# One block around both layers, ordered with TimelineSim: a two-layer graph network on one core

## The chip, the cores and the metric

The kernel runs on one core of one Trainium2 chip. The metric is device time in microseconds of one execution. Five engines work in parallel, each through its own instructions in order: TensorE (PE, with its weight loads PEld), VectorE (DVE), ScalarE (ACT), GpSimd (POOL) and SyncE (SP). PE writes to PSUM, and the other engines move its results on. An engine whose next instruction waits for a semaphore holds up everything behind it in its own order.

## The reference, cut to what matters

The input x is 32 batches of 512 tokens with 256 features, adj a 0/1 matrix of 512 x 512 per batch, all float32 or int32. Two layers, each a graph step and a feed-forward step, each on a layer norm and added to its input:

```python
# layer 0
h = x @ W_msg;  msg = adj.T @ h / max(deg, 1)
x = x + relu(x @ W_upd + msg + bias)
t = max over features of (xf + Wt[u]) + bt          # 1024 outputs u
trop = s * max_p(t*sl_cvx + of_cvx) + (1-s) * min_p(t*sl_ccv + of_ccv)
out = (g*trop + (1-g)*gelu(xf @ Wc + bc)) @ Wd + bd # g = sigmoid(xf @ Wg + bg)
# layer 1
attention of 4 heads over adj;  x = x + norm(relu(att @ h + bias) + h)
sw = softmax((x @ W_x.T) @ W_slice.T / temp)        # 8 heads x 64 slices
st = (fx.T @ sw) / (sum(sw) + 1e-5)                 # 64 slice tokens of 512 features
ot = bidirectional state-space scan over the 64 slice tokens
x = x + (ot spread back by sw) @ out_w.T
```

(In the last lines x stands for the normed x where the reference norms it.)

## The kernel before, in words

`tile_kernel` (L2158) traces the whole program. Python generators yield after small pieces of work, and `woven` (L66) and a credit in layer 1 (L1595) interleave them, so that pieces of several batches are traced alternately. The traced order isn't yet the order of execution: the Tile scheduler takes the traced instructions of a block as a list in order of priority, runs them through a simulation of the machine, and writes for each engine the order in which that simulation issued them. Buffers of a pool and semaphores follow from that order. The kernel before gives no block of its own around the layers, so the scheduler's standard simulation orders them.

**Layer 0** is `layer0_sorted` (L98). In the front, about 330 us long, `features` prepares sorted weights while the first graph steps run. A graph step of one batch is `conv_in` (L386: ph L404) and `conv_out` (L412: pu L424, pm L434, and keep, the rows written for later). After every 8 batches (a segment of 4096 tokens), `put_in_order` (L473) sorts the tokens by how many features can decide their max-plus. `feed_forwards` (L543) then handles each segment in 8 groups of 512 sorted tokens, 32 groups in all: indirect DMAs on POOL gather the tokens (xs, L553) and rows of a table (L564, L595), DVE does the max-plus (L598), PE transposes xs and does clsp and gatep (L623), ACT turns them into cls and gate (L625), PE transposes the maxima (tz, L630), ACT and DVE build acc from tz (L632, L636, L637 to L641), and PE multiplies acc down (po, L652). The tiles clsp and gatep have two PSUM buffers between them, as do po with the graph steps, the transposes of xs, and tz. The graph steps of the next segment are woven in, and behind the last segment the setup and the first steps of layer 1.

**Layer 1** is `layer1_plain` (L865), with two streams.

- `attentions`: `prepare(b)` (L1148) gathers a batch, norms it, transposes it (x3T), computes heads (hp, L1180) and writes one row per head to DRAM (ownd, L1197, on SP), from where it is loaded to all partitions (own, L1200, on SP). `attention(b)` (L1216) forms the weights att on DVE (L1213) from own, other and mask, and multiplies them on PE (avp L1249, adp L1254); then norms the result (L1282 to L1300; mu goes through a power on POOL).
- `mixer(g)` for 16 groups of two batches. `slices` for each batch: lgp (L1335) and sw on ACT and DVE (L1336 to L1342), yTp (L1347), swp (L1352). `tokens` for both: uTp (L1366), rnp (L1372), scale on ACT (L1375), uT on DVE (L1379, L1381). `scan`: xp (L1400), bcp (L1409), dtp (L1428), zp (L1393); a convolution and activations on DVE and ACT; gp (L1487), segp (L1491, from seg, with decay = exp of it on ACT, L1493), xtp (L1496, copied to xk, L1498), qp (L1501); mix on DVE (L1505 to L1510); yp (L1517), y (L1522), yTp (L1527), yT (L1529), oTp (L1535), vp (L1557). `unslice`: outp (L1567), and the store of the batch.

The mixer of one group is one long chain of dependent steps through PE, ACT and DVE. Its counterpart, the attention of later batches, is traced between its steps by this credit:

```python
for want in mixer(g):
    credit += want * PACE
    while credit >= 1.0:
        credit -= 1.0
        if next(ahead, True):
            credit = 0.0
```

att has 13 buffers, own 5, x 5; the PSUM pool of layer 1 has 4 buffers for each of two tags (any for most, pv for the attention). After both layers come a sum of flags (L2196 to L2204) and a conditional branch to a general version of the layers, which isn't taken with these data.

Of the kernel before, what the change touches and what calls it, by code (L numbers as in the profile page):

```python
# [2156 lines left out]
@with_exitstack  # L2157
def tile_kernel(ctx, tc, ins, out):  # L2158
    nc = tc.nc
    cst = ctx.enter_context(tc.tile_pool(name="cst", bufs=1))  # L2160
    dram = ctx.enter_context(tc.tile_pool(name="dram", bufs=1, space=DRAM))
    ident = cst.tile([P, P], F32, tag="ident", name="ident")
    make_identity(nc, ident)
    eps = cst.tile([P, 1], F32, tag="eps", name="eps")
    nc.gpsimd.memset(eps, LN_EPS)
    eps2 = cst.tile([P, 2], F32, tag="eps2", name="eps2")
    nc.gpsimd.memset(eps2[:, 0:1], LN_EPS)
    nc.gpsimd.memset(eps2[:, 1:2], -0.5)

    def group(prefix):  # L2170
        return {k[len(prefix):]: v for k, v in ins.items() if k.startswith(prefix)}

    w0 = group("L0_gnn_") | group("L0_ffn_")
    w1 = group("L1_gnn_") | group("L1_ffn_")
    w1["gnn_bias"] = ins["L1_gnn_bias"]
    x2 = [dram.tile([N, D], F32, tag=f"x2_{b}", name=f"x2_{b}") for b in range(ins["x"].shape[0])]
    n0 = len(x2) * NT + w0["Wt"].shape[0] // P
    n1 = len(x2) * NT + 2 * w1["W"].shape[0] + 3
    again = cst.tile([1, 1], I32, tag="again", name="again")
    with tc.tile_pool(name="few", bufs=1) as few:  # L2180
        over = few.tile([P, n0 + n1], F32, tag="over", name="over")
        NSEG = 4
        x2s = [dram.tile([len(x2) // NSEG * N, D], F32, tag=f"x2s_{i}", name=f"x2s_{i}") for i in range(NSEG)]
        ranks = few.tile([P, len(x2) * NT], I32, tag="ranks", name="ranks")
        rest = []

        def following(ps):
            rest.append(layer1_plain(tc, ident, eps2, x2s, ranks, ins["adj"], w1, out, over[:, n0:], ps))
            return iter(lambda: next(rest[0]), True)

        layer0_sorted(tc, ident, eps2, ins["x"], ins["adj"], w0, x2s, ranks, over[:, :n0], following)
        for _ in rest[0]:
            pass


        ones = few.tile([P, 1], F32, tag="ones", name="ones")  # L2196
        nc.gpsimd.memset(ones, 1.0)
        worst = few.tile([P, 1], F32, tag="worst", name="worst")
        nc.vector.tensor_reduce(worst, over, AX.X, ALU.add)
        with tc.tile_pool(name="pf", bufs=1, space=PSUM) as ps:  # L2200
            pf = ps.tile([P, N], F32, tag="flag", name="flag")
            nc.tensor.matmul(pf[:1, :1], worst, ones, start=True, stop=True)
            nc.vector.tensor_copy(again, pf[:1, :1])
    rows = nc.values_load(again, min_val=0, max_val=4 * P * (n0 + n1))  # L2204
    with tc.If(rows > 0):
        layer0(tc, ident, eps, ins["x"], ins["adj"], w0, x2)
        layer1(tc, ident, eps, x2, ins["adj"], w1, out)
# [32 lines left out]
```

## Time and profile before

| | |
|---|---|
| median of 3 runs | 4462.75 us (4462.54 to 4462.93) |
| the profiled execution | 4459.08 us |
| its span on the core | 4456.4 us, so 2.7 us lie around it |
| mean granted TensorE clock | 0.948 of full speed |
| front, 0 to 330 us | PE busy 194.8 us |
| DMA over the span | 474.21 MB, mean 106 GB/s |
| layer 1's POOL mu L1300, 32 times | 111.6 us busy, 391.1 us idle before it for DVE |
| layer 0's DVE best L598, 212 times | 274.4 us busy, 121.9 us idle before it, most for ACT best L592 |

The profile shows one execution. A line of its timeline gives start and length in us, the engine, the line of the code, the operation, the tiles written and read, their shape and how often it stands in a run; the bracket behind it gives the idle time before it and what ended that. A line of the waits gives who waited for whom, the total in us, how often, and the longest.

### The profile page before, as it was taken

How to read it: one execution, taken by the hardware profiler on the slowest of the kernel's cores; microseconds unless marked ns; L12 is line 12 of the kernel's file. 1: busy time of each engine (PE TensorE's matmuls, PEld its weight loads, DVE VectorE, ACT ScalarE, POOL GpSimd, SP SyncE). 2: the span in 40 equal slices, each digit the busy share in tenths (PEclk: the TensorE clock that was granted, in tenths of full speed). 3: DMA queues.
4: the chain of work that ended last, by engine and by line, in shares of the span. 5: the costliest groups of instructions: out<-in, count | busy, mean ns of one | idle time of the engine just before them, and what ended most of it. 6: DMA issues, size and time to landing. Idle time of an engine off the chain costs nothing.

```text
span 4456.4 us, 57911 instructions
## 1 busy us (share of the span) xinstructions
PE 3922.0 (88%) x20311; PEld 2470.6 (55%) x20311; DVE 3347.2 (75%) x7008; ACT 2291.6 (51%) x4756; POOL 1718.8 (39%) x2036
## 2 busy tenths in 40 slices
PE   5568898899988999888997899999999999999987
PEld 4454565566656656545554455555555555555555
DVE  6668887897788987877766777767677877778763
ACT  3345565566564665556654544544545444454433
POOL 2357644664446644454314232332222232332220
PEclk8679999999999999989998999999999999999998
DMA  5546543664436543564422111111111111111100
GB/s 133 160 144 223 190 130 122 210 200 139 156 117 213 187 147 129 162 201 167 138 81 67 36 53 57 56 48 58 51 43 42 53 55 55 58 48 58 41 15 16
DMA packets 235107, 474.21 MB, mean 106 GB/s; under 512 B 38299, under 2 KB 114075, under 8 KB 234804
## 3 DMA queue, kind: packets, MB, share of 16 engines
q0 software_dynamic: 98688, 315.94, 22.2%
q1 hardware_dynamic: 136116, 154.46, 11.0%
q8 instruction: 162, 2.65, 0.2%
q14 instruction: 141, 1.16, 0.1%
HBM read 413.16 MB, written 57.16 MB: 106 GB/s over the span
## 4 chain that ended last, share of the span: by engine, by line
DVE 34%; PE 32%; DMA 11%; issue 9%; POOL 9%; ACT 5%; SPq 0%; POOLq 0%; DVEq 0%; ACTq 0%
DVE att L1213 5%; DVE acc L637 4%; PE clsp L623 3%; PE avp L1249 3%; PE po L652 3%; PE gatep L623 3%; DMA rows<-table,xs 2%; PE yTp L1347 2%; DVE sw L1337 2%; DVE sw L1342 2%; DVE best L598 2%; DMA rows<-table,tops 2%; DVE sst L1340 2%; DMA best<-table,xs 2%; PE xp L1400 1%
## 5 line engine op out<-in xcount | busy, mean ns | idle before, releaser
L623 PE MATMUL clsp<-xnT,wc 128*128 128x512 f32 x1024 | 520.8, 627 | 49.7 <-ACT cls L625 37.6
L623 PE MATMUL gatep<-xnT,wg 128*128 128x512 f32 x1024 | 499.8, 607 | 10.5 <-ACT gate L625 7.7
L652 PE MATMUL po<-wd,acc 128*128 128x256 f32 x2048 | 455.4, 381 | 6.1 <-DVE acc L641 3.8
L1213 DVE SCALAR_TENSOR_TENSOR att<-own,other,mask 128x512 f32<-128x512 f32 x512 | 392.9, 796 | 79.0 <-DMA own<-ownd 79.0
L652 PEld LDWEIGHTS po<-wd,acc 128*128 128x128 f32 x2048 | 388.3, 191 | 72.1 <-issue 9.2
L598 DVE SCALAR_TENSOR_TENSOR best<-rows,xs,best 128x1024 f32<-128x1024 f32 x212 | 274.4, 1295 | 121.9 <-ACT best L592 76.4
L637 DVE SCALAR_TENSOR_TENSOR acc<-past,fld,acc 128x512 f32<-128x512 f32 x448 | 345.7, 775 | 24.9 <-ACT past L636 16.9
L632 ACT ACTIVATE acc<-tz,fld 128x512 f32<-128x512 f32 x256 | 198.8, 777 | 269.3 <-PE tz L630 240.1
L623 PEld LDWEIGHTS gatep<-xnT,wg 128*128 128x128 f32 x1024 | 196.0, 196 | 252.3 <-issue 197.9
L636 ACT ACTIVATE past<-tz,fld 128x512 f32<-128x512 f32 x448 | 291.4, 693 | 68.1 <-DVE acc L637 66.6
L1347 PE MATMUL yTp<-sw,x 128*128 128x512 f32 x512 | 264.6, 655 | 64.3 <-DVE sw L1342 59.6
L595 POOL DMA_INDIRECT rows<-table,xs x212 | 249.5, 1177 | 171.6 <-DVE best L598 119.0
L1249 PE MATMUL avp<-att,hv 128*32 128x512 f32 x2048 | 298.9, 607 | 5.6 <-DVE att L1213 5.6
L623 PEld LDWEIGHTS clsp<-xnT,wc 128*128 128x128 f32 x1024 | 181.5, 198 | 188.1 <-issue 111.8
L434 PE MATMUL pm<-h,adj 128*128 128x258 f32 (+1 forms) x1024 | 181.2, 324 | 99.9 <-DVE keep L427 33.7
L1300 POOL TENSOR_TENSOR mu<-mu,eps 128x16 f32<-128x16 f32 x32 | 111.6, 3487 | 391.1 <-DVE mu L1299 391.0
L1335 PE MATMUL lgp<-wsl,x4T 128*128 128x512 f32 x512 | 242.8, 613 | 15.7 <-ACT sw L1336 6.8
L1154 POOL DMA_INDIRECT x<-x2s,ranks x128 | 135.9, 1062 | 298.1 <-DVE att L1213 148.1
L625 ACT ACTIVATE gate<-gatep,fld 128x512 f32<-128x512 f32 x256 | 175.5, 685 | 142.6 <-PE gatep L623 123.8
L553 POOL DMA_INDIRECT xs<-rows_of,order x128 | 156.1, 1219 | 221.5 <-DVE acc L637 100.8
L1567 PE MATMUL outp<-v,swT 128*128 128x256 f32 x1024 | 227.6, 381 | 0.0
L625 ACT ACTIVATE cls<-clsp,fld 128x512 f32<-128x512 f32 x256 | 176.1, 688 | 93.9 <-PE clsp L623 55.6
(599 smaller groups left out, 8978.1 us busy)
## 6 DMA issues: line engine op xcount, KB each, us to landing
adj<-in_adj POOLq DMA_DIRECT2D x128, 256.0 KB
ai<-in_adj SPq DMA_DIRECT2D x128, 256.0 KB
own<-ownd SPq DMA_DIRECT2D x128, 256.0 KB
rows_of<-keep SPq DMA_DIRECT2D x32, 550.0 KB
x<-in_x SPq DMA_DIRECT2D x32, 512.0 KB
x2s<-xs SPq DMA_DIRECT2D x32, 512.0 KB
out<-x SPq DMA_DIRECT2D x32, 512.0 KB
rows<-table,xs POOLq DMA_INDIRECT x212
```

Of the source, the lines that this page charges most:

```text
L595: nc.gpsimd.indirect_dma_start(out=row, out_offset=None, in_=table, in_offset=bass.IndirectOffsetOnAxis(ap=idxs[:, k : k + 1].bitcast(U32) ...
L598: nc.vector.scalar_tensor_tensor(m, row, vals[:, k : k + 1], m, ALU.add, ALU.max)
L623: nc.tensor.matmul(pf, wf[:, c, f * P : (f + 1) * P], xnT[:, c, :], start=c == 0, stop=c == DC - 1)
L625: nc.scalar.activation(o, pf, fn, bias=fld[:, f, bf : bf + 1], scale=1.0 if fn == AF.Gelu else 0.5)
L636: nc.scalar.activation(r, z, AF.Relu, bias=fld[:, f, AT + b : AT + b + 1])
L637: nc.vector.scalar_tensor_tensor(y, r, fld[:, f, CH + b : CH + b + 1], y, ALU.mult, ALU.add)
L652: nc.tensor.matmul(po[:, i, :], acc[f][:, t * P : (t + 1) * P], wd[:, f, :], start=f == 0, stop=f == FC - 1)
L1213: nc.vector.scalar_tensor_tensor(e, own[h], other[:, j, h : h + 1], mask[:, j, :], ALU.max, ALU.mult)
L1249: nc.tensor.matmul(pv[p][k * HW : (k + 1) * HW, :], hv[:, j, h, e : e + HW], weighed[b, h, j], **ends)
L1335: nc.tensor.matmul(pf, xnT[:, c, t * P : (t + 1) * P], wsl[:, c, :], start=c == 0, stop=c == DC - 1)
L1347: nc.tensor.matmul(py, xn[:, t, c * P : (c + 1) * P], sw[:, t, :], start=t == 0, stop=t == NT - 1)
L1567: nc.tensor.matmul(po[:, :D], swT[:, k, t * P : (t + 1) * P], v[:, k, :], start=k == 0, stop=k == KC - 1)
```

## The change: a block with another simulation

Both layers are traced inside one `tc.block`, which tells the scheduler to order it with TimelineSim, its more detailed simulator, in place of the standard one. What is traced, and in which order, is the same. The setup ahead of it (constants, the DRAM tiles) and the sum of flags behind it lie outside the block.

```diff
-        layer0_sorted(tc, ident, eps2, ins["x"], ins["adj"], w0, x2s, ranks, over[:, :n0], following)
-        for _ in rest[0]:
-            pass
-
+        with tc.block(schedule_with_timeline_sim=True):
+            layer0_sorted(tc, ident, eps2, ins["x"], ins["adj"], w0, x2s, ranks, over[:, :n0], following)
+            for _ in rest[0]:
+                pass
```

## The prediction

> **What bounds the kernel now.** I read the page's busy line first, then the chain, then busy time by stage, then what PE waits for in the steady part of layer 1, then single stretches of PE's timeline. From the page, and from the table by stages (columns: length, PE busy, PEld, DVE, ACT, POOL, PE clock, DMA share, GB/s):
>
> ```profile
> PE 3922.0 (88%) x20311; PEld 2470.6 (55%) x20311; DVE 3347.2 (75%) x7008; ACT 2291.6 (51%) x4756; POOL 1718.8 (39%) x2036
> DVE 34%; PE 32%; DMA 11%; issue 9%; POOL 9%; ACT 5%; SPq 0%; POOLq 0%; DVEq 0%; ACTq 0%
> ```
>
> ```profile
> 330.00:2375.00 2045.00, 1843.23 (x7181) 1181.03 (x7179) 1655.47 (x3053) 1198.60 (x2019) 1017.15 (x1254) 0.96 0.49 159
> ...
> 2534.00:4300.00 1766.00, 1643.19 (x10865) 985.75 (x10868) 1304.62 (x2811) 862.22 (x2205) 508.07 (x390) 0.98 0.16 50
> ```
>
> PE is the bound: layer 0 leaves it 2045.0 - 1843.2 = 202 us idle, the steady part of layer 1 only 1766.0 - 1643.2 = 123 us, about 9 us per group of two batches (the group from 3036.4 to 3162.7 takes 126.3 us, with PE busy for 116.8). The chain is spread over all engines, so PE's idle time is made of many short waits. No matmul is removed or added; so an order can only change these idle stretches, and the clock that follows them. PE's largest waits from 2560 to 4200, 13 groups (us in total, times, longest):
>
> ```profile
> PE yTp L1347 <- DVE sw L1342: 55.3, 31, 3.0
> PE oTp L1535 <- ACT yT L1529: 13.3, 14, 1.1
> PE rnp L1372 <- DVE mu L1293: 9.8, 12, 2.7
> ```
>
> The mixer's long chain (rnp, uT, xp, conv, gp, mix, yp, y) hardly appears here, because attention matmuls of the next batch stand between its hops. The last group has no next batch, so it shows the bare hops (start, length, and in brackets the idle time before):
>
> ```profile
> 4386.63 1.15 PE L1372 MATMUL rnp<-ident,rn 128*64 128x64 f32 x32
> 4390.43 5.44 PE L1400 MATMUL xp<-uT,inT 128*128 128x128 f32 x32 [2.65 <-DVE uT L1381]
> ...
> 4399.80 3.68 PE L1393 MATMUL zp<-inT,uT 128*128 128x512 f32 x8
> 4407.84 0.45 PE L1487 MATMUL gp<-cpad,bcT 64*64 64x64 f32 x8 [4.36 <-issue]
> 4408.23 1.87 PE L1491 MATMUL segp<-seg,seg_l 128*64 128x512 f32 x4
> ...
> 4416.13 3.28 PE L1517 MATMUL yp<-xk,mix 64*64 64x64 f32 x32 [3.48 <-DVE mix L1510]
> ```
>
> The same steps in a steady group have no idle before them and are shorter:
>
> ```profile
> 3162.67 3.84 PE L1400 MATMUL xp<-uT,inT 128*128 128x128 f32 x32
> ...
> 3180.01 0.46 PE L1487 MATMUL gp<-cpad,bcT 64*64 64x64 f32 x8
> 3180.39 1.42 PE L1491 MATMUL segp<-seg,seg_l 128*64 128x512 f32 x4
> ...
> 3188.86 1.90 PE L1517 MATMUL yp<-xk,mix 64*64 64x64 f32 x32
> ```
>
> **The change part by part.** I compared the built programs, engine by engine. The counted instructions and DMAs are the same one for one; 16 of 104 activation table loads go, each engine gets two branches, and waits are merged differently (more wait instructions on PE, DVE and ACT). So this is purely a question of order. I take the work between two steps in each order and price it by the rows of before.
>
> *Layer 1, per group.* In the new order nearly all attention matmuls of the group's second batch (about 25 us of PE work) stand ahead of uTp, inside the stretch where PE waited for sw; before, they stood behind it, between the mixer's hops. From this:
>
> - rnp to xp: filler 3.4 us before, none after (1.4 in every third group). The bare hop is 2.65 idle, so +2.65 or +1.25, on average 2.2.
> - zp to gp and segp: filler 6.6 before, 0.8 after. In the last group segp starts 12.36 us after xp's end (4395.87 to 4408.23); in a steady group zp ends 7.6 us after it (3166.51 to 3174.12). That leaves 4.75, less 0.8 filler and 0.46 for gp: 3.5. The new ACT order has one table load less here (1.28): 2.2. I take 2.8.
> - qp to yp: filler 5.8 before, 3.8 after, against a bare 3.48. The filler would cover it, but part of it is hp of the next batch, whose inputs are ACT copies now queued behind decay and xk. Ends 0 and 3.5; I take 2.0.
> - clock: in the last group xp takes 5.44 for 3.84 (+1.60), segp, xtp and qp 4.69 for 3.04 (+1.65), yp 3.28 for 1.90 (+1.38), at granted clocks 0.66 to 0.50. That is 4.6 if every hop lowers the clock and 0 if none does; I take half, 2.3.
> - own rows: att of the second batch (L1213) now stands on DVE ahead of half of the first's sw steps (L1337 to L1342). DVE waits at att for the DMA own<-ownd, 73.9 us in 13 groups, 5.7 each, so far with little of PE's behind it; now sw, and with it yTp, are queued behind. The queue on SP keeps its order. Ends 0 and 5.7; I take 4, since about half of sw has still to be done when the rows land.
> - saved: the waits for sw, 55.3 + 2.7 (L1341) over 13 groups, 4.5 each; and yTp, which took 7.56 us for 4.56 after such a wait in some groups (at clock 0.62), half of 3.0. Together 6.0. At the low end 7.5, at the high end 0, if the matmuls that fill the gap wait for own themselves.
>
> Sum: 2.2 + 2.8 + 2.0 + 2.3 + 4.0 - 6.0 = +7.3 per group, over 15 groups with a next batch +110 us. All low ends give 1.25 + 2.2 - 7.5 = -4.0, or -60 us; all high ends +20, or +300, which would need every bound at once.
>
> On the clock, the rows say this: gaps of 2.65 and 2.87 us were followed by 0.66 and 0.62, another gap of 2.87 by full speed (yTp in 4.56 us at 2771); hence the half. The Trainium skill, "TensorE: Matmul & The Clock Gate", section "Why this matters for your kernels", asks for no idle gaps over about 3 us between bursts; by that rule only the 3.48 and 4.36 gaps would cost clock, and xp's half of 1.60 would drop out, 0.8 per group or 12 us of the sum. The gap of 2.65 that was followed by 0.66 speaks against it.
>
> *Layer 0.* Transposes of xs come about 50 us earlier on PE, clsp and gatep about 5 us later, po is interleaved with them instead of standing in one run, and ACT does acc and past of some slices ahead of cls and gate of the next. PE waits at clsp and gatep for ACT, 37.1 + 9.5 + 7.7 = 54 us, and at tz for ACT 15 us from 330 to 2300: at best these 69 us go. At worst every one of the 32 groups of tokens pays one acc and past pair (0.78 + 0.69) at both buffers of clsp/gatep, 2.9 us, or 94. I take 0, near the middle, as the trace shows both cases.
>
> *Front and edges.* Until 330 us DVE's features and conv steps are reshuffled by -21 to +13 us, and one weight's load moves behind small ones. The nearest row is PE's wait pm for keep, 31.8 us: ends -32 and +32, taken as 0. Branches: the launch has only 2.7 us outside its span, so a few us at most, taken as 0. The 16 table loads (1.28 us each, 20 us) are hidden: ACT is busy for 51%. Without that cover, in the conv section alone, the load is already in the segp term.
>
> The Trainium skill, "ScalarE: Activation LUTs", section "What ACT_TABLE_LOAD costs", adds 1.38 us of drain to each load, which would make the 16 loads worth 43 us instead of 20. In the last group the load at 4398.18 ends at 4399.46 and the ACTIVATE starts at 4399.48, so this trace shows no such drain behind it.
>
> Against the profiled execution, 4459.1 us (span 4456.4 and 2.7 around it): 4459 + 110 = 4569. The median shown is 3.7 above that execution, so 4573.
>
> **The rivals.**
>
> *A, faster.* The waits that PE has now are filled with work that is ready, and the hops are short, because DVE and ACT reach uT, seg and mix with less queued ahead. Saved 6.0 per group against hops at their low ends, 1.25 + 2.2: -2.5, or -38 us; layer 0 gains half of its 69: -35. 4459 - 73 + 4 = 4390. It decides wherever hops, clock and own cost less than 6.0 us per group. For it: DVE rests a quarter of the time, the hops' steps are 0.2 to 0.7 us each. Against it: the bare hops of the last group were measured with nothing queued ahead and still took 2.65 to 4.4.
>
> *B, layer 0 pays too.* As the forecast, and clsp waits for its two buffers in each group of tokens: + 94, so 4667. For it: ACT's past and acc run further ahead in the new order. Against it: the pair of cls and gate is still issued per slice.
>
> *C, no difference.* Waits move from sw to the hops and cost the same, 6 for 6; layer 0 as before: 4463, within 0.2% (9 us, about what a measurement of this kernel can tell from no change). The orders differ widely, so exact balance is luck. That the block isn't reordered at all is excluded by the lists.
>
> **How the numbers follow.** Forecast (4500 to 4640) 0.50; B (above that) 0.16; A 0.29; C 0.05. Predicted is the forecast's 4573. The range leaves out about 0.1 on each side: from 4420, into A's half, to 4680, past B. Slower 0.66, same 0.05, faster 0.29. The forecast's own range is 4500 to 4640.
>
> **What would show it.** In the profile after, PE's waits from 2560 to 4200 should list xp for uT at 1 to 2.7 us a time, segp or gp for seg at 2 to 4, yTp for sw less than 55 us; the group's period should be 133 us instead of 126; DVE att waiting for own with sw behind it. Layer 0 should keep about 202 us of PE idle. I am wrong if the period is under 126 (the hops were covered, A), or if layer 1 keeps its period and layer 0 moves by over 50 us.

## The result and the profile after

The changed kernel takes 4764.1 us (median of 4 runs, 4758.2 to 4779.7), the kernel before 4462.8 us (4 runs): a ratio of 1.068, 95% interval 1.065 to 1.070. It is slower by 301 us; the prediction had the sign, at 110 us, and its range ended at 4680.

The profiled execution took 4758.2 us, its span 4756.4. The same views as before: the page's busy line and chain, and the table by stages (length, PE busy, PEld, DVE, ACT, POOL, PE clock, DMA share, GB/s) with layer 0 up to its last po and the steady part of layer 1:

```profile
PE 4067.3 (86%) x20311; PEld 2526.2 (53%) x20311; DVE 3388.8 (71%) x7008; ACT 2287.0 (48%) x4740; POOL 1740.1 (37%) x2036
PE 19%; DVE 15%; ACT 6%; DMA 5%; POOL 3%; issue 3%; SPq 0%; POOLq 0%; ACTq 0%; DVEq 0%
```

```profile
330.00:2381.00 2051.00, 1859.09 (x7271) 1203.26 (x7269) 1675.03 (x3122) 1223.00 (x2053) 1064.40 (x1291) 0.96 0.50 160
2600.00:4600.00 2000.00, 1759.14 (x10599) 1014.71 (x10595) 1330.52 (x2758) 837.56 (x2145) 495.98 (x384) 0.95 0.14 44
```

The counts of PE's matmuls are the same, yet PE is busy for 145 us more. Layer 0 leaves it 192 us idle, about as before (202). In layer 1 the idle share of PE rises from 7% to 12%. The first xp of each group dates the stages: from the 1st to the 15th, 14 groups take 125.05 us each before and 144.10 after. That is 14 x 19.05 = 267 of the 300 us of span. Another 30 lie ahead of the first xp (2533.9 against 2563.5: 6 up to layer 0's last po, 23 from there to the first xp) and 4 behind the 15th.

PE's waits in the steady part (us in total, times, longest):

```profile
PE xp L1400 <- DVE uT L1381: 43.1, 11, 3.9
PE yTp L1347 <- DVE sw L1342: 39.4, 32, 3.2
PE gp L1487 <- ACT z L1450: 28.5, 8, 4.9
PE segp L1491 <- DVE seg L1481: 22.2, 8, 4.8
PE hp L1180 <- ACT swT L1353: 17.2, 18, 1.3
PE segp L1491 <- ACT z L1450: 14.5, 4, 4.6
```

The hops of the mixer are now in the list, as predicted, and longer than in the last group of before; yTp still waits for sw. One steady group of after, the hops (start, length, idle before in brackets):

```profile
3286.84 5.44 PE L1400 MATMUL xp<-uT,inT 128*128 128x128 f32 x32 [3.94 <-DVE uT L1381]
...
3305.46 0.70 PE L1487 MATMUL gp<-cpad,bcT 64*64 64x64 f32 x8 [4.90 <-ACT z L1450]
3306.09 1.97 PE L1491 MATMUL segp<-seg,seg_l 128*64 128x512 f32 x4
...
3308.91 1.71 PE L1501 MATMUL qp<-fcT,xT 128*128 128x8 f32 x8
...
3315.21 1.90 PE L1517 MATMUL yp<-xk,mix 64*64 64x64 f32 x32
```

xp, gp and segp run behind gaps of 3.94 and 4.90 us, and slower: xp takes 5.44 us against 3.84 in the steady group of before, segp 1.97 against 1.42, and the granted clock over segp, xtp and qp is 0.50. In one point this group isn't typical: the four matmuls of segp stand together in it. In the other 13 of the 14 steady groups xtp, and mostly also qp and transposes, stand between the first two and the last two, and segp takes 3.4 us of PE in the mean of all 14, against 1.3 before, where the four are together in every group. Why uT's gap is 3.94 and not 2.65 stands on DVE: a row of the attended batch's norm lies between uT's two steps:

```profile
3283.83 1.13 DVE L1379 SCALAR_TENSOR_TENSOR uT<-uTp,bfx_eps,scale 128x128 f32<-128x128 f32 x4 [1.29 <-ACT scale L1375]
3284.87 1.22 DVE L1303 TENSOR_TENSOR av<-av,mu 128x1024 f32<-128x1024 f32 x1
3286.01 0.69 DVE L1381 TENSOR_TENSOR uT<-uT,bfx 128x512 f32<-128x512 f32 x1
```

But the hops are the smaller part. These are lgp and the first yTp of the group's first batch, on PE before:

```profile
3221.60 5.37 PE L1335 MATMUL lgp<-wsl,x4T 128*128 128x512 f32 x12
3227.53 0.38 PE L1084 MATMUL maskp<-identb,a 128*128 128x128 bf16 x4 [0.56 <-DVE mask L1085]
3229.52 1.98 PE L1335 MATMUL lgp<-wsl,x4T 128*128 128x512 f32 x4 [1.61 <-ACT sw L1336]
...
3235.30 1.88 PE L1347 MATMUL yTp<-sw,x 128*128 128x512 f32 x4
```

and after:

```profile
3353.53 1.98 PE L1335 MATMUL lgp<-wsl,x4T 128*128 128x512 f32 x4
3355.45 1.49 PE L1249 MATMUL avp<-att,hv 128*32 128x512 f32 x11
...
3356.76 0.61 PE L1249 MATMUL avp<-att,hv 128*32 128x512 f32 x3
...
3357.30 3.70 PE L1335 MATMUL lgp<-wsl,x4T 128*128 128x512 f32 x8
...
3363.01 1.98 PE L1335 MATMUL lgp<-wsl,x4T 128*128 128x512 f32 x4
...
3374.45 2.49 PE L1347 MATMUL yTp<-sw,x 128*128 128x512 f32 x4 [3.23 <-DVE sw L1342]
```

Attention matmuls now stand between the four quarters of lgp, in short pieces, and PE still waits 3.23 us for sw at the end: 13.7 us from lgp to yTp became 20.9. This is one of the two longest cases; over the 14 groups the mean goes from 13.8 to 18.0. On DVE a batch's statistics and the norm of an attended batch stand ahead of sw. Its rows there in after:

```profile
3360.84 0.43 DVE L1126 BATCH_NORM_STATS2 stc<-x 128x6 f32<-128x256 f32 x1 [1.21 <-DMA x<-x2s,ranks]
...
3362.61 3.38 DVE L1303 TENSOR_TENSOR av<-av,mu 128x1024 f32<-128x1024 f32 x1 [0.53 <-POOL mu L1300]
3365.91 0.68 DVE L1337 TENSOR_TENSOR sw<-sw,ebsl 128x512 f32<-128x512 f32 x1
...
3373.66 1.24 DVE L1342 TENSOR_TENSOR sw<-sw,sst 128x512 f32<-128x512 f32 x2
```

The 3.38 us of L1303 are an exception too: 4 of its 32 rows in after take that long, two of them in the 14 groups, and the others 1.22.

In the second batch of the group the order on DVE changed more. From the last sw step on, PE and DVE before:

```profile
3266.35 3.83 PE L1347 MATMUL yTp<-sw,x 128*128 128x512 f32 x8
...
3271.33 3.60 PE L1347 MATMUL yTp<-sw,x 128*128 128x512 f32 x8
3268.29 0.69 DVE L1342 TENSOR_TENSOR sw<-sw,sst 128x512 f32<-128x512 f32 x1
3268.90 4.84 DVE L1213 SCALAR_TENSOR_TENSOR att<-own,other,mask 128x512 f32<-128x512 f32 x4
```

and after, with more of sw still to come:

```profile
3402.29 1.88 PE L1347 MATMUL yTp<-sw,x 128*128 128x512 f32 x4
...
3413.54 1.98 PE L1347 MATMUL yTp<-sw,x 128*128 128x512 f32 x4
3399.45 1.29 DVE L1342 TENSOR_TENSOR sw<-sw,sst 128x512 f32<-128x512 f32 x2
3401.96 0.75 DVE L1213 SCALAR_TENSOR_TENSOR att<-own,other,mask 128x512 f32<-128x512 f32 x1 [1.22 <-DMA own<-ownd]
...
3406.58 3.35 DVE L1213 SCALAR_TENSOR_TENSOR att<-own,other,mask 128x512 f32<-128x512 f32 x5
...
3411.32 0.69 DVE L1342 TENSOR_TENSOR sw<-sw,sst 128x512 f32<-128x512 f32 x1
...
3412.58 0.69 DVE L1342 TENSOR_TENSOR sw<-sw,sst 128x512 f32<-128x512 f32 x1
```

Before, sw is done when att begins. After, 12 rows of att (of the next group's second batch) stand ahead of the third quarter of sw and a 13th ahead of the fourth, and PE fills the time with attention. It is so in all 14 groups: between the first and the last sw step of the second batch lie 13 rows of att, 9.7 us, and 1.2 us of waiting for own; before it was 2.2 rows and 3.0 us. From its first step to its last sw takes 18.9 us there instead of 11.3, and in the first batch 15.8 instead of 12.9.

From these I drew up PE's account of a mean group (14 groups, from the trace), in two parts: the hops, from uTp to outp, and the slices of both batches, from outp to the next uTp. Each microsecond is attention (avp, adp), the mixer's own matmuls, other matmuls, or idle.

| us per group | attention | mixer | other | idle | sum |
|---|---|---|---|---|---|
| hops, before | 12.1 | 27.8 | 6.2 | 2.1 | 48.2 |
| hops, after | 0.6 | 32.5 | 7.1 | 10.0 | 50.2 |
| slices, before | 10.9 | 48.6 | 10.8 | 6.7 | 76.9 |
| slices, after | 27.1 | 48.0 | 11.6 | 7.2 | 93.9 |

Half of the attention (92 of its 192 records in a group; the trace has two records for each matmul of the program; 11.5 us) has left the hops. They became no shorter, since idle and slow matmuls took its place. It went into the slices, and filled nothing there: their idle time is as long as before, and the attention itself takes 4.7 us more. The account shows where the time stands, not yet what causes it.

### The profile page after: what moved, and what is told of

It reads as the page before. It is cut to its first block, busy times and chain, and to the rows that moved or that the text cites. A ratio compares the mean times of both kernels' runs of the same rounds, so it can differ in the third digit from the quotient of the medians.

```text
span 4756.4 us, 58270 instructions
## 1 busy us (share of the span) xinstructions
PE 4067.3 (86%) x20311; PEld 2526.2 (53%) x20311; DVE 3388.8 (71%) x7008; ACT 2287.0 (48%) x4740; POOL 1740.1 (37%) x2036
## 3 DMA queue, kind: packets, MB, share of 16 engines
q8 instruction: 162, 2.65, 0.2%
## 4 chain that ended last, share of the span: by engine, by line
PE 19%; DVE 15%; ACT 6%; DMA 5%; POOL 3%; issue 3%; SPq 0%; POOLq 0%; ACTq 0%; DVEq 0%
DVE att L1213 4%; PE yTp L1347 3%; PE hp L1180 2%; DMA own<-ownd 2%; PE avp L1249 2%; POOL x L1154 2%; DMA x<-x2s,ranks 2%; PE adp L1254 1%; PE lgp L1335 1%; PE oTp L1535 1%; DVE sw L1337 1%; ACT x L1133 1%; PE segp L1491 1%; DVE sst L1340 1%; DVE sw L1342 1%
## 5 line engine op out<-in xcount | busy, mean ns | idle before, releaser
L623 PE MATMUL clsp<-xnT,wc 128*128 128x512 f32 x1024 | 504.9, 615 | 35.2 <-ACT cls L625 21.8
L652 PE MATMUL po<-wd,acc 128*128 128x256 f32 x2048 | 474.1, 383 | 27.1 <-DVE acc L641 18.1
L1213 DVE SCALAR_TENSOR_TENSOR att<-own,other,mask 128x512 f32<-128x512 f32 x512 | 354.8, 749 | 95.9 <-DMA own<-ownd 93.1
L1249 PE MATMUL avp<-att,hv 128*32 128x512 f32 x2048 | 345.4, 605 | 12.2 <-DVE att L1213 11.8
L553 POOL DMA_INDIRECT xs<-rows_of,order x128 | 144.0, 1125 | 464.9 <-DVE acc L637 285.7
L1300 POOL TENSOR_TENSOR mu<-mu,eps 128x16 f32<-128x16 f32 x32 | 94.0, 2937 | 494.6 <-DVE mu L1299 461.9
L1348 ACT COPY yT<-yTp 128x512 f32<-128x512 f32 x64 | 37.5, 586 | 441.2 <-PE yTp L1347 441.2
```

The source lines that it names most:

```text
L623: nc.tensor.matmul(pf, wf[:, c, f * P : (f + 1) * P], xnT[:, c, :], start=c == 0, stop=c == DC - 1)
L652: nc.tensor.matmul(po[:, i, :], acc[f][:, t * P : (t + 1) * P], wd[:, f, :], start=f == 0, stop=f == FC - 1)
L1213: nc.vector.scalar_tensor_tensor(e, own[h], other[:, j, h : h + 1], mask[:, j, :], ALU.max, ALU.mult)
L1249: nc.tensor.matmul(pv[p][k * HW : (k + 1) * HW, :], hv[:, j, h, e : e + HW], weighed[b, h, j], **ends)
```

## The experiments

The theories at the start were **hops** (the bare hops of the mixer cost the time) and its rival **sw** (VectorE's order makes sw late, and TensorE's order puts attention ahead of the chain in the slices). Later came a third, **busy** (the short pieces of attention and the slow matmuls cost the time by themselves). All rules below are order rules without a semaphore:

```diff
+def behind(ins, other):
+    tc.add_manual_dep(ins.ins, other.ins.name,
+        mybir.DependencyInfo(mybir.DependencyClass.NoSync, mybir.DependencyReason.DATA), reason="order")
```

Where a run is single, its time is read beside the spread of the kernel before in one series, 4449 to 4476 us over 13 runs; differences under 20 us of single runs aren't read.

**e1_block_standard**: the block, but with the standard simulation.

```diff
-        with tc.block(schedule_with_timeline_sim=True):
+        with tc.block():
```

> The block stays, but the standard simulation orders it; the order on PE is that of the kernel before, with two more branches. Theory 'order' (the loss comes from the order alone): 4460 to 4470 us, as before. Rival 'block' (the block's edges, its branches and the merged waits cost by themselves): clearly above 4470, at the extreme near 4760.

Measured 4463.5 us (before beside it 4460.0). The block costs nothing that shows; the order that TimelineSim gives is the whole change.

**e2a_bare_xp** (before, with the first quarter of the second batch's attention moved behind zp) and **e2b_bare_hops** (before, with that batch's attention, both traced and executed, behind yp):

```diff
+        def hop(b, j, ins):
+            if b % GB and j == 0 and 1 in marks.get((b - 3) // GB, {}):
+                behind(ins, marks[(b - 3) // GB][1])
...
-            tok_matmul(pz, 0, DI)
+            marks[g][1] = marks[g][2] = tok_matmul(pz, 0, DI)
```

```diff
+            while b % GB and b > GB and (b - 3) // GB not in marks:
+                yield True
...
+            marks[g] = mark
             y = inner(f"y{g}")
```

> The kernel before, with one rule for PE: the first turn of the second batch's attention matmuls stands behind zp, so that nothing but 4 mask transposes covers the hop from rnp to xp (in most groups). Theory 'hops': xp waits 2.6 to 3.9 us for uT and then takes 5.4 instead of 3.8 us: 4 to 5.5 us for each of some 13 groups, 4515 to 4540 us. Rival 'elsewhere' (DVE's order and the split attention make the loss, and a gap at xp is given back because the moved matmuls fill another gap): within 15 us of 4463.

> The kernel before, with the second batch's attention matmuls of each group put behind yp on PE, so that all three hops of the mixer stand as bare as in the kernel after, while the other engines are ordered by the standard simulation. Theory 'hops': xp idle 3.5 and segp/gp idle 4.9 us per group, slower clock on xp, segp, xtp and qp 4.9 us: 13 us per group and more, the period from 125 to 138 us or more, 4640 to 4730 us in all. Rival 'elsewhere': under 4540 us.

Measured 4503.9 and 4700.8 us. One bare hop costs 2.7 us per group (125.05 to 127.73). The prediction's terms for it give 3.0, 2.2 of idle time and xp's half of 1.60; e2a was expected at 4 to 5.5, so its time lies below the range of the theory and above that of the rival. e2b gave the predicted time, but not for the expected reason. Its hops from xp to yp take 28.9 us instead of 26.0; 12 of the 15.7 us per group appear between outp and lgp (+5.0) and between the batches' swp and lgp (+7.0), where the moved attention went. Removing a filler costs its hop, and the filler costs again where it lands.

**e3_hops_filled**: after, with the four quarters of the second batch's attention behind rnp, zp, zp and qp, the places they have before (the *hop rule*).

```diff
+        def hop(b, j, ins):
+            if b % GB and j in marks.get((b - 3) // GB, {}):
+                behind(ins, marks[(b - 3) // GB][j])
```

> The kernel after, with four rules for PE: the turns of the second batch's attention matmuls stand behind rnp, zp, zp and qp of the group, so that the hops are covered again; everything else is left to the detailed simulation. Theory 'hops': 13 of the 19 us per group come back, period 144 to 131 us, about 4570 us. Rival 'elsewhere' (att ahead of sw on DVE, the yTp wait and the split attention): the period stays above 139 us, over 4690 us.

Measured 4748.9 us. The hops' idle time falls from 10.0 to 4.8, and the slices' idle time rises from 7.2 to 12.9: yTp now waits for sw for longer. In the steady part of e3 the waits read:

```profile
PE yTp L1356 <- DVE sw L1351: 119.9, 47, 7.8
PE xp L1411 <- DVE uT L1391: 19.0, 10, 3.1
```

So **hops** alone fell: with attention out of the slices, PE stands and waits there for sw.

**e4_sw_first, e5_both_rules, e7_sw_first_before**: the *sw rule* puts the att of a group's second batch on DVE behind the last sw step of the second batch of the group before (`b - GB`), whose sw it had held up. e4 is after with it, e5 after with it and the hop rule, e7 the kernel before with it.

```diff
+                one = nc.vector.scalar_tensor_tensor(e, own[h], other[:, j, h : h + 1], mask[:, j, :], ALU.max, ALU.mult)
+                if b % GB and b - GB in swept:
+                    behind(one, swept[b - GB])
...
+                swept[b] = nc.vector.tensor_mul(s, s, st.unsqueeze(2).to_broadcast([P, H, G]))
```

> The kernel after, with one rule for DVE: att of the second batch of a group (L1213) stands behind the group's last sw step, so that the wait for the own rows no longer holds sw up. Theory 'two bounds' (in the kernel after, the bare hops and the late sw each bound the mixer's chain, and mending one alone exposes the other): yTp's wait for sw falls from 3.3 us per group (9.7 with the hops filled) to under 2, a part of the attention slides behind rnp, and the hop at zp to segp stays bare; period 144 to between 134 and 140, 4610 to 4700 us. Rival 'hops alone': still 4740 to 4770. Rival 'sw alone': period under 130, below 4570.

> The kernel after, with the four rules that fill the hops on PE and the rule that puts sw first on DVE. Theory 'two bounds': now the 13 us of the hops and the 9 us of late sw both go; period 126 to 130, 4490 to 4550 us, with layer 1's start still about 25 us late. Rival 'ACT or memory' (what remains is ACT's order in the convolution, or PSUM buffers): the period stays above 135, over 4630 us.

> The kernel before, with the rule for DVE alone: sw first, then att of the second batch. In the kernel before, yTp waits 4.4 us per group for sw, and att waits 5.7 us for own on DVE with a part of sw behind it. Theory: 2 to 4 us per group go, 4400 to 4440 us. Rival (yTp's wait is set by sw's own steps of 2.3 us per quarter, not by att ahead of them): 4455 to 4470 us.

Measured 4693.2, 4600.7 and 4449.2 us; 139.8, 134.2 and 124.5 us per group. The gains of the two rules don't add: 0.1 us per group for the hop rule alone, 4.3 for the sw rule alone, 9.9 together. e5 is half the way back, short of the 4490 to 4550 that was expected, and e7 gained less than its 4400 to 4440. With the rule, sw of the second batch takes 8.7 us from its first step to its last (18.9 in after). What remains is in the slices (80.4 us against 76.9) and the hops (53.9 against 48.2).

**e6_turns_whole, e8_all_rules, e9_all_rules_before**: the theory **busy**. The 12 matmuls of one quarter of attention are chained, so that nothing comes between them; e6 is after with that, e8 is e5 with it, e9 the kernel before with all three rules.

```diff
+                    with tc.high_priority():
+                        one = None
+                        for p in reversed(range(AP)):
...
+                                one = chain(one, nc.tensor.matmul(
```

> The kernel after, with one thing mended: the 12 attention matmuls of a turn (24 records in the trace) start only when the last of their four att tiles is there and stay together on PE, ahead of other ready work; the hops stay bare. In the traces so far an attention record costs 0.12 us in runs of 16 and more, 0.16 in runs of 8 to 15 and 0.3 to 0.46 in shorter ones, and the kernel after has 12 runs per group where the kernel before has 8. Theory 'split': avp and adp go from 27.7 us busy per group to 23 or 24, and as PE's work stands in the chain ahead of uTp, the period falls by 4 to 5 us, 4690 to 4710 us. Rival 'covered' (the chain waits for DVE there, so shorter PE work is lost in the wait): 4740 to 4770.

> The kernel after with all three: hops filled, sw first on DVE, turns whole. Theory 'split': from 134.2 us the period falls to 129 or 130, 4525 to 4550 us. Rival 'covered': 4590 to 4610, as with the two rules.

> The kernel before, standard simulation, with the same three rules. If the rules name what the standard order already does, this stays near the kernel before, 4440 to 4465 us, and what then lies between it and the kernel after with the same rules is what the detailed simulation orders badly elsewhere (ACT, the front, layer 1's start). If the rules themselves cost time, it is above 4480.

Measured 4744.0, 4645.8 and 4561.9 us. In e6 the matmuls of the slices' attention take 21.3 us instead of 27.1, and the period stays (144.9): the slices' idle time grows from 7.2 to 13.8. The same two groups of after and of e6, 2600 to 4500 (busy, mean ns):

```profile
L1249 PE MATMUL avp<-att,hv 128*32 128x512 f32 x1674 | 284.0, 606 | 10.9 <-DVE att L1213 10.8
L1254 PE MATMUL adp<-att,hv 128*32 128x512 f32 x832 | 176.9, 597 | 0.0
```

```profile
L1259 PE MATMUL avp<-att,hv 128*32 128x512 f32 x1712 | 202.1, 602 | 13.4 <-DVE att L1213 13.2
L1264 PE MATMUL adp<-att,hv 128*32 128x512 f32 x864 | 102.9, 593 | 1.9 <-DVE av L1285 1.9
```

PE's busy time per matmul falls by 30 to 44% and the group gains nothing: PE's idle time before yTp rises from 3.3 to 8.4 us per group, so it isn't PE that ends last there, but sw. The rule has a cost of its own, as it holds a quarter back until its last att tile is there. e8 is 2.9 us per group slower than e5, outside both of its ranges, and e9, with all three rules, 7.3 us per group slower than before; which of the three costs it there wasn't taken apart. **Busy** fell as far as the attention rows go.

**e10_chain_clear**: e5, with the first batch's last two quarters of attention kept behind swp and lgp too.

```diff
+            if b % GB == 0 and j == 2 and b - GB in turned_at:
+                behind(ins, turned_at[b - GB])
+            if b % GB == 0 and j == 3 and (b - 1, 2) in weighted:
+                behind(ins, weighted[b - 1, 2])
```

> The kernel after with hops filled, sw first, and two more rules on PE: of the first batch's attention, turn 2 stands behind the last swp of the slices before and turn 3 behind the third quarter of lgp, about where the kernel before has them. New theory 'chain' (the mixer is one serial chain, group after group, since sw and v share one buffer; attention matmuls that stand in a stretch of it where PE itself is next lengthen it by their whole time, in a hop where ACT and DVE work they are free): with two rules 8.4 us of the 9.2 us that are left per group lie between outp and the first yTp; some 6 us of them go, period 127 to 130, 4500 to 4545 us. Rival 'hops' (gaps and slower clock make the loss, wherever attention stands): within 15 us of 4601.

Measured 4590.1 us, 133.1 per group: a miss. The attention in the slices falls by 1.4 us and the idle time rises by 1.6; yTp waits for sw again, 73.5 us in 25 times, now in the first batch. Clearing TensorE is of no use while sw is late.

**e11_zp_twice** and **e12_uTp_twice**: after, with the matmuls of zp, then of uTp, done twice in each group.

```diff
             tok_matmul(pz, 0, DI)
+            tok_matmul(pz, 0, DI)
```

```diff
-                    for c in range(DC):
+                    for c in [*range(DC)] * 2:
```

> The kernel after, with zp's matmuls done twice (the same result written again): 3.5 us more work for PE per group, 53 us in all, in the bare hop between zp and gp; the order is otherwise the same. Theory 'chain': the hop is ACT's and DVE's, so the added work is free, within 10 us of 4764; if the slow clock behind the gap is in the chain, segp, xtp and qp get faster and up to 3 us per group come back, 4720. Rival 'PE work' (PE is the bound, every matmul counts): 4810 to 4820.

> The kernel after, with uTp's matmuls done twice (the same result written again): 1.9 us more work for PE per group, in a stretch of the chain where PE is next. Theory 'chain': the whole of it counts, +28 us or so, 4785 to 4800. Rival 'idle time' (PE has 17 us of idle time per group that take it up): within 8 us of 4764.

Measured 4722.4 and 4772.4 us. e11 does 3.5 us more on PE in each group, and each group is 2.2 us **shorter** (141.86). The second zp fills most of the wait of gp for z, and the clock stays up. This is the same group as the steady one of after above, and PE has the same order in both:

```profile
3288.78 7.11 PE L1393 MATMUL zp<-inT,uT 128*128 128x512 f32 x16
...
3298.04 0.46 PE L1488 MATMUL gp<-cpad,bcT 64*64 64x64 f32 x8 [1.47 <-ACT z L1451]
3298.72 1.08 PE L1492 MATMUL segp<-seg,seg_l 128*64 128x512 f32 x4 [0.23 <-DVE mask L1085]
...
3300.22 0.96 PE L1502 MATMUL qp<-fcT,xT 128*128 128x8 f32 x8
...
3305.54 1.90 PE L1518 MATMUL yp<-xk,mix 64*64 64x64 f32 x32
```

The granted clock over segp, xtp and qp is 1.00 for 0.50, they take 2.46 us for 4.53, and from gp to yp it is 7.50 us for 9.75. So in this group the slow clock behind this one hop is on the path, for about 2.3 us. In the other 13 the scheduler ordered the hop anew as well: in e11 the four matmuls of segp stand together in all 14 groups. e12 has no second zp, but has segp together in 8 groups, and its stretch from xp to yp is 3.2 us shorter than that of after (25.6 for 28.8). How much of e11's 2.2 us per group is clock, and how much is order, isn't shown. The Trainium skill, "TensorE: Matmul & The Clock Gate", section "Why this matters for your kernels", asks for no idle gaps over about 3 us; here the gaps of 3.94 and 4.90 were followed by slow matmuls, and 1.47 by fast ones, which agrees; the 2.65 of the last group of before, followed by 0.66, does not. e12 was inconclusive: it was to price work in the chain (28 us expected) and took 8 us, within the spread of after. The period stayed (144.08), as its own stretch grew by 2.7 us per group and the one from xp to yp shrank by the 3.2.

**e14 to e17, crossover**: the kernel after, in which one engine's whole order, or two, is forced to that of the kernel before, by chaining its instructions; the scheduler still orders the rest.

```diff
+        queue = [traced[n] for n in (f"I-{k}" for k in names) if n in traced]
+        for one, two in zip(queue, queue[1:]):
+            tc.add_manual_dep(two, one.name, mybir.DependencyInfo(mybir.DependencyClass.NoSync, mybir.DependencyReason.DATA), reason="order")
```

> The kernel after, but VectorE's whole order is forced to that of the kernel before; the scheduler with TimelineSim still orders the other engines around it. Theory (the late sw on VectorE and attention ahead of the chain on TensorE carry the 19 us per group together, and once sw is early TimelineSim itself puts most of TensorE's attention back between the hops): period 126 to 133 us per group instead of 144.1, time 4510 to 4610. Rival 1 (TensorE's order carries it): period above 139, time above 4690. Rival 2 (ScalarE's order carries it): likewise above 4690.

> The kernel after, but TensorE's whole order is forced to that of the kernel before. Theory: the hops are filled again, but sw stays late on VectorE, so yTp waits and everything behind it on TensorE with it: period 133 to 142, time 4610 to 4730. Rival 1 (TensorE's order carries the loss): period below 130, time below 4560. Rival 2 (ScalarE's order): about as the kernel after, above 4740.

> The kernel after, with TensorE's and VectorE's whole orders forced to those of the kernel before; ScalarE, GpSimd and SyncE stay as TimelineSim orders them. Theory: period 125 to 128, time 4465 to 4530. Rival 2 (ScalarE's, GpSimd's or SyncE's order carries a good part): period above 132, time above 4590.

> The kernel after, but ScalarE's whole order is forced to that of the kernel before. Theory: ScalarE's order costs little by itself, period 141 to 146, time 4715 to 4790. Rival 2 (ScalarE's order carries the loss: copies of heads and x3T queued behind decay and xk, z late for gp): period below 136, time below 4650.

Measured 4715.1, 4890.9, 4599.4 and 4903.5 us. Every one is later at the first xp than after itself (2636, 2692, 2612 and 2691 us against 2563.5). That a forced order meets other engines' new ones in layer 0 is likely, but wasn't followed. So all four whole times missed what was expected, and by the times alone e14, e15 and e16 would speak for the rivals; the period of a group in layer 1 is compared instead:

| order of before on | us per group | attention in hops | idle in hops | attention in slices | idle in slices |
|---|---|---|---|---|---|
| none (after) | 144.1 | 0.6 | 10.0 | 27.1 | 7.2 |
| DVE (e14) | 136.2 | 11.0 | 5.6 | 19.0 | 4.4 |
| PE (e15) | 145.3 | 12.3 | 3.7 | 11.8 | 19.8 |
| PE and DVE (e16) | 129.8 | 12.1 | 3.6 | 11.6 | 7.9 |
| ACT (e17) | 145.2 | 0.7 | 10.5 | 27.0 | 6.4 |
| all (before) | 125.1 | 12.1 | 2.1 | 10.9 | 6.7 |

This settles the main cause in the groups, though my periods for three of the four runs were off by 2 to 4 us, e14's between the theory and the rival. TensorE's order alone brings nothing: the hops are filled, and all of it comes back as the wait for sw. In the steady part of e15:

```profile
PE yTp L1347 <- DVE sw L1342: 176.9, 47, 8.2
```

VectorE's order alone brings 7.9 us, and the scheduler then puts most of TensorE's attention back into the hops by itself. Both bring 14.3 of the 19.05. ScalarE's order alone brings nothing, which excludes the rival that e15's period, about that of after, would have fitted. The last 4.7 us hang on what is still new beside these two, the orders of the other engines and queues and the buffers that follow from them; in e16 the largest new waits are

```profile
PE lgp L1335 <- DVE mask L1085: 29.0, 6, 6.0
PE maskp L1084 <- DVE mask L1085: 18.7, 7, 3.5
```

47.7 us in 13 groups or 3.7 each, for the masks of a later batch. What holds those up I didn't follow; it stays open.

**e13_sw_first_before_5**: e7 again, for an interval.

> The kernel before with sw first on DVE, the fastest version so far, timed in rounds. By the theory 'chain' yTp of the second batch comes a little earlier: the one look gave 4449, 0.26% under the kernel before; 4445 to 4455 again. If that was chance: 4460 to 4468.

4449.8 us (median of 9) against 4464.2 (13 runs), a ratio of 0.9977, interval 0.9961 to 0.9994: the sw rule in the standard order is faster than both kernels, by 0.23%. In the one execution with a trace that is 1.1 us per group (123.98), where e1, with the order of before, has 124.71.

## Why the prediction was right in its sign and wrong in its size

The working, term by term, per group; "measured" is the difference in PE's account, after less before:

| step | predicted | measured |
|---|---|---|
| idle in the hops (xp 2.2, segp and gp 2.8, yp 2.0) | +7.0 | +7.9 (xp 3.8, segp and gp 4.9, yp -0.1, the rest -0.7) |
| mixer matmuls of the hops ("clock", "I take half") | +2.3 | +4.7 (xp 1.7, segp 2.1, xtp and qp 1.0, yp 0, the rest -0.1) |
| idle in the slices: own rows +4.0, saved -6.0 | -2.0 | +0.5 |
| attention matmuls themselves | not priced | +4.7 |
| other matmuls, and the mixer's in the slices | not priced | +1.2 |
| sum | +7.3 | +19.0 |

**The step that failed is "saved": "the waits for sw, 55.3 + 2.7 (L1341) over 13 groups, 4.5 each ... Together 6.0.", and with it the size of "own rows", 4.0.** "Saved" took the moved attention as filler for the wait at sw. A wait for another engine's product is filled only if that product comes no later. Here DVE's order was changed as well. The prediction did name the mechanism, att ahead of sw on DVE, but priced it by the wait for own alone and put att's own time there at nothing. In the runs it is the other way round: in the second batch of each group 1.2 us of that wait lie within sw, and 9.7 us of att for 3.0 before, so sw takes 18.9 us for 11.3. (It is the sw of the second batch of the group before that is held up, not "the first's".) In the first batch, between 3360 and 3366, DVE does a batch's statistics, waiting for gathered rows (DMA), and a norm row waiting for POOL, ahead of sw; there sw takes 15.8 us for 12.9. So the wait moved on about as far as what was put in front of it: PE still idles 3.3 us per group before yTp, for 4.4 before, after 16 us more of attention in the slices, and the slices' idle time didn't fall by 2.0 but rose by 0.5. e3 and e15 show the gain failing to appear (attention out of the slices, wait longer), e4 and e14 show that DVE's order brings it back, and e16 that it takes both.

**The second is the attention itself.** "No matmul is removed or added; so an order can only change these idle stretches, and the clock that follows them." The order also changed how matmuls stand together, and the attention took 4.7 us more on PE. e6 shows that this was under cover of sw in after: removed alone, it brings nothing. As far as e6 goes, it is a size of the account, and not a cause of the time.

**The clock** was sized at half of 4.6, and the account has 4.7, but that they are so near is luck. xp lost its 1.6 whole, xtp and qp 1.0, and yp nothing of its 1.38. segp lost 2.1, and most of this is order: together and at the slow clock it takes 1.97 us, 0.7 more than before, but with its matmuls apart 3.4 in the mean. The account's number isn't the path's, either: in the one group that e11 leaves in the same order on PE, the slow clock behind the longest hop cost 2.3 us; the other hops' share stays open. xp's gap grew to 3.94 us because DVE put 1.22 us of norm between the two steps of uT; this I hadn't looked for. The rule of 3 us, weighed in the prediction, would have taken 0.8 from the term, as it stood on a gap of 2.65 us; with the gap that came, it agrees with the slow xp.

**The hops' idle time** was right to 13%, but in other places: qp to yp stayed covered (0 for 2.0), while gp and segp wait 4.9 us for z and seg instead of 2.8. e2a is near the price of one bare hop: 2.7 for 2.2 and 0.8 of clock.

**Own rows**: from 2600 to 4300 us DVE waits at att for own for 72.8 us before and 76.2 after. With 1700 / 125.05 = 13.6 and 1700 / 144.10 = 11.8 groups in that stretch, these are 5.4 and 6.5 us per group, so the wait itself hardly grew. The time of att itself, and what is queued behind it, was the point; e4 prices that, 4.3 us per group.

**Layer 0** was taken as 0 and took 6 us up to its last po; PE's idle time of 192 us is near the 202 foretold. Between that and the first xp lie 23 us that I priced at nothing: this is the start of layer 1, and what costs it there stays open. No run takes the 16 table loads by themselves; with ACT's old order (e17) the period stayed at 145.2, so no worth of theirs shows.

Rival A (faster, waits filled with ready work) failed where the forecast's own "saved" did, and its hops, taken at 3.45 us, measured 7.9. Rival B's time (4667) was the nearest, but by another cause. The high ends gave +20 per group, "which would need every bound at once", and that 19 was measured is no proof of them: yp's 3.5 didn't come, the idle time before xp and gp went beyond its bounds, and 4.7 us of the sum are attention that wasn't priced. The general mistake of size was to add hops and slices as independent idle sums.

## What to carry to other kernels

When an order is changed on several engines, a gap on one of them is not room for work until the step that ends it has been followed back on the engine that makes it, in the new order; list what stands ahead of that step there, with its own time and not only its waits, before the gap is counted as saved. Draw the account of one period in two parts, where work leaves and where it lands, and charge it in both. To find which engine's order carries a loss, give one engine its old order whole and watch the period and the waits: two old orders that bring nothing and 8 of 19 us alone brought 14 together here.

## What the hardware showed beyond that

More work on TensorE went with a faster kernel: with 3.5 us of needless zp per group the period fell by 2.2 us. In the group that kept its order on PE, segp, xtp and qp behind it took 2.46 us instead of 4.53, at a granted clock of 1.00 instead of 0.50; in the others the order changed too.

The attention matmuls, which write 32 columns each, cost PE by how many stand together. A run's time, divided by its records in the trace, is 0.11 to 0.14 us in runs of 16 or more, 0.16 in runs of 8 to 15, and 0.41 in runs under 8 (in after, where 31 of 169 runs are under 8, and 25 of these have two records, at 0.52 each; before, 15 of the 16 such runs have 5 to 7 records, at 0.18). Three of them, between others, took 0.60 us, where 16 in a run took 1.92 in a steady group of before:

```profile
3352.99 0.60 PE L1254 MATMUL adp<-att,hv 128*32 128x512 f32 x3
```

A DVE row of 128x1024 that takes 1.22 us elsewhere took 3.38 (L1303 at 3362.61), while POOL worked on a tile of the same size:

```profile
3362.57 2.34 POOL L1167 TENSOR_TENSOR x<-x,beta 128x1024 f32<-128x1024 f32 x1
```

Both rows start within 0.05 us of each other. All four rows of L1303 that took 3.36 us or more in after began within 0.07 us behind such a row of L1167, and none of its other 28 ran beside one. No run here took the one away, so that POOL is the reason is not shown.
